# Two graph layers over a dense adjacency: layer 1's product with h by seven block products in place of eight

## The chip, the cores and the metric

The kernel runs on one core of a Trainium2 chip. The metric is the device time of one launch in microseconds (us): the median of three timed runs. One more execution was profiled; its times come from the hardware profiler. Engines: PE (TensorE, with PEld for its weight loads), DVE (VectorE), ACT (ScalarE), POOL (GpSimd), SP (SyncE, which here only issues DMAs).

## The reference, cut to what matters

16 batches of 1024 nodes with 128 features; adj is 1024 x 1024 per batch, float32. Layer 0 is one attention with a softmax and three gates; layer 1 has four heads.

```python
# layer 1, per head: h = X @ conv_w + conv_b  (1024 x 128)
scores = jnp.einsum('hbni,hij,hbmj->hbnm', h, attn_w, h)
Ah = jnp.tanh(A[None] * scores)
hh = jax.nn.relu(jnp.einsum('hbnm,hbmd->hbnd', Ah, h))   # the product with h
Xm = jax.nn.relu(jnp.mean(hh, axis=0))
return jax.nn.relu(Xm + X)
# both layers: x = layernorm(x + layer(x))
```

## The kernel before

All is float32. The main loop (L890) goes over the batches b, and for each over 32 **steps**: step = 8 * head + m, where m is a block of 128 source nodes.

Layer 1, one step (`layer1_step`, L694). PE makes the scores of block m against all 1024 target nodes in two tiles of 512 (L711, by `halves_mm`, L138, which splits a product into two of 64 weight columns). They land in PSUM buffers of the pool `ps_sc`, four deep, which all of layer 0's small products share. DVE multiplies each tile with the adjacency into `s` (L712), and ACT takes the tanh of the step's 1024 columns (L713). The product with h (`back`, L715 to L732) adds h[m]^T s into the PSUM tile `acc`, as eight products of 64 weight columns by 256 moving columns; it is issued two steps after its scores (`push`, DELAY = 2). At m = 7 `add_head` adds relu(acc) to `sum` on DVE (L745, L747).

Layer 0 of later batches is cut into named pieces, which two tables lay between the steps: BETWEEN (L872) ends layer 0 of batch b + 1, AHEAD (L877) begins that of batch b + 2. A piece's instructions go into each engine's queue after those of the step, and every queue runs in order. The pieces that matter here, with their DVE or POOL work:

- Lj loads the adjacency's block j; Ej makes its mask (POOL, L408, two buffers); Aj masks row j and takes its maximum (DVE, L425 to L433), then the exponential (ACT); Bj divides, multiplies with the adjacency (DVE, L451, L458) and issues the product of row j - 1 (`weigh`, `back`, L445 to L471).
- Sj makes scores (PE, ACT), Tj turns a row of them (DVE, then a DRAM round trip on SP: `hop`, L265).
- F, i, o are the gates (DVE reductions, POOL products with `wu_b`); I0 and O0 are eight small DVE operations each (L592, L603); V0 has the layer norm's statistics (DVE, L218 to L221) and then a power on POOL (L222); N0 normalises (DVE, L233). `turn_x1` then turns x1 for the next batch.

In a batch b >= 1, V0 stands at step 23, N0 at 24, `turn_x1` at 25, A0 to A2 at 29 to 31, and the rest of A and B in steps 31 and 0 to 10. At step 31 PE also makes the next batch's uT (`head_uT`) and half of its rows of h (`rows`, L677), which ACT copies out of `ps_sc`; at step 0 the other half. `layer1_end` finishes the output of the batch before at the steps ENDING. The adjacency of a batch is loaded once, for both layers (16 buffers).

Of the kernel before, what the change touches and what calls it, by code (L numbers as in the profile page):

```python
# [19 lines left out]
P = 128  # L20
EPS = 1e-5
# [3 lines left out]
def two_layer_adjacency_kernel(  # L25
# [28 lines left out]
    adjp = ctx.enter_context(tc.tile_pool(name="adjp", bufs=2 * NB))  # L54
    sb = ctx.enter_context(tc.tile_pool(name="sb", bufs=2))
    ps_sc = ctx.enter_context(tc.tile_pool(name="ps_sc", bufs=4, space=PSUM))
# [7 lines left out]

    warm = sb.tile([P, N], F32, tag="sum", name="warm", bufs=1)
    nc.vector.memset(warm[:, :P], 0.0)
    ident = consts.tile([P, P], F32, name="ident")
# [4 lines left out]
    a_in = sb.tile([P, P], F32, tag="hz", name="a_in", bufs=4)  # L72
    nc.scalar.dma_start(a_in, A)
    ww_in = sb.tile([P, P], F32, tag="hz", name="ww_in", bufs=4)
# [3 lines left out]
    rows_x = sb.tile([3, P], F32, tag="s1", name="rows_x", bufs=4)  # L78
# [35 lines left out]
    cw_in = sb.tile([P, H, D], F32, tag="s1", name="cw_in", bufs=4)  # L114
    cw_last = sb.tile([P, H, D], F32, tag="s1", name="cw_last", bufs=4)
    aw = sb.tile([P, H, D], F32, tag="s1", name="aw", bufs=4)
    cw = consts.tile([P, H, D], F32, name="cw")
    cwT = sb.tile([P, H, P], F32, tag="s1", name="cwT", bufs=4)
    caT = sb.tile([P, H, P], F32, tag="s1", name="caT", bufs=4)
# [4 lines left out]
    a_sym = sb.tile([P, P], F32, tag="hz", name="a_sym", bufs=4)  # L124
    s_ww = sb.tile([P, P], F32, tag="hz", name="s_ww", bufs=4)
# [3 lines left out]
    b_wide = sb.tile([P, P], F32, tag="uT1", name="b_wide")  # L129
# [7 lines left out]

    def halves_mm(out, lhsT, rhs, start, stop):  # L138
        for c in range(2):
            nc.tensor.matmul(out[ts(c, 64)], lhsT[:, ts(c, 64)], rhs, start=start, stop=stop)  # L140
# [33 lines left out]
    def join_weights():  # L174

        nc.gpsimd.memset(cw_last[0:1], 0.0)
        nc.gpsimd.tensor_sub(cw, cw_in, cw_last)
        yield
        pt = small("p_cwT")
        for hd in range(H):  # L180
            nc.tensor.transpose(pt[:, ts(hd, P)], cw[:, hd, :], ident)
        nc.scalar.copy(cwT.rearrange("p h f -> p (h f)"), pt)
        yield
        pt = small("p_caT")
        for hd in range(H):
            nc.tensor.matmul(pt[:, ts(hd, P)], aw[:, hd, :], cwT[:, hd, :], start=True, stop=True)
        nc.scalar.copy(caT.rearrange("p h f -> p (h f)"), pt)  # L187
        yield
        pt = small("p_m")
        for hd in range(H):  # L190
            nc.tensor.matmul(pt[:, ts(hd, P)], caT[:, hd, :], cwT[:, hd, :], start=True, stop=True)
        nc.scalar.copy(ms.rearrange("p h f -> p (h f)"), pt)
# [10 lines left out]
    def layernorm(t, dst, name, on_scalar=False, eps=EPS, own=False):  # L203
# [17 lines left out]
        nc.vector.tensor_scalar_add(rs, mv[:, :, 1], eps)  # L221
        nc.gpsimd.tensor_tensor(rs, rs, mhalf[:, :n], ALU.pow)  # L222
# [15 lines left out]
    def project_T(dst, w, src, bias, name, halves=range(NH), split=True):  # L238

        for q in halves:  # L240
            ps = small(f"pT_{name}_{q}")
            (halves_mm if split else nc.tensor.matmul)(
                ps, w, src[:, ts(q, 512)], start=True, stop=True
            )
            if bias is None:
# [3 lines left out]

    def project_rows(dst, w, src, bias_row, name):  # L250

        for q in range(NH):
            ps = small(f"pR_{name}_{q}")
            psv = ps.rearrange("p (k d) -> p k d", d=D)
            for k in range(BH):
                nc.tensor.matmul(psv[:, k, :], src[:, ts(q * BH + k, P)], w, start=True, stop=True)
            nc.vector.tensor_add(
                dst[:, q * BH : (q + 1) * BH, :], psv,
                bias_row.unsqueeze(1).to_broadcast([P, BH, D]),
            )  # L260
# [18 lines left out]

    def land():  # L280
        while hops:
            hops.popleft()()
# [6 lines left out]

    adj_t, x1_t, x1T_t = {}, {}, {}  # L290


    def layer0(b):
# [6 lines left out]
        mm = halves_mm if b else nc.tensor.matmul  # L300

        def load_xT():
            t["xT"] = sb.tile([P, N], F32, tag="xT", name=f"xT_{b}")
            nc.sync.dma_start(t["xT"], xT[b])

        def load_adj(j):
            a = adj_t[b, j] = adjp.tile([P, N], F32, tag="adj", name=f"adj_{b}_{j}")

            (nc.sync if b < 2 else nc.gpsimd).dma_start(a, adjT[b, ts(j, P), :])  # L309
# [5 lines left out]
        def project_q(q):  # L315
# [7 lines left out]
            if (b, q) != (0, 0):  # L323
                return project_T(t["qT"], q_w, t["xT"], c_col, f"q0_{b}", [q], split=b > 0)
# [76 lines left out]
        def find_edges(j):  # L401

            if b == 0:
                m = sb.tile([P, N], BF16, tag="h1", name=f"edge_{b}_{j}", bufs=NB + 1)
# [3 lines left out]
            engine.tensor_scalar(m, adj_t[b, j], 0.0, None, ALU.is_gt)  # L408
# [36 lines left out]
        def weigh(j):  # L445

            s = row(j)
            adj = adj_t[b, j].rearrange("p (k d) -> p k d", d=P)
            rz = sb.tile([P, 1], F32, tag="rz", name=f"rz_{b}_{j}", bufs=4)
            t["hz", j] = sb.tile([P, D], F32, tag="hz", name=f"hz_{b}_{j}", bufs=4)  # L450
# [8 lines left out]
            if j and (b or j not in (1, NB - 1)):  # L459
                back(j - 1)  # L460

        def back(j, halves=range(NH)):
            if j == 0:
                acc = ps_acc.tile([P, N], F32, tag="acc0", name=f"acc0_{b}")

                other = ps_acc.tile([P, N], F32, tag="acc1", name="acc_other") if b == 0 else acc
                t["acc"] = [acc[:, :512], other[:, 512:]]
# [11 lines left out]
        def relu():  # L479
            back(NB - 1)  # L480
            for q in range(NH):
                relu_half(q)
# [12 lines left out]
        def rows_half(q):  # L495
# [3 lines left out]
            pt = ps_acc.tile([P, N], F32, tag=f"acc{q}", name=f"pt0_{b}_{q}")  # L499
# [74 lines left out]
        def gate_f():  # L574
            sum_hp(1)
            sigmoid(t["gate"][:, :, 1:2])
            forget()
# [22 lines left out]
        def outer(p):  # L600
# [6 lines left out]
            t["norm", p] = layernorm(u[:, ks], t["x1"][:, ks, 1 : D + 1], f"0_{b}_{p}")  # L607
# [21 lines left out]
        else:  # L629
            pieces.update(R=relu, P=turn_hp, Y=partial(weigh_hp, 1), F=gate_f, i=gate_i, o=gates_io)  # L630
# [45 lines left out]

    def rows(b, ks):  # L677

        for k in ks:
            h1_t[b, k] = sb.tile([P, H * D], F32, tag="h1", name=f"h1_{b}_{k}", bufs=NB + 1)  # L680
            ps = small(f"pR1_{b}_{k}")
            halves_mm(
                ps, x1T_t[b][:, ts(k, P)], cw.rearrange("p h d -> p (h d)"), start=True, stop=True
            )
            nc.scalar.copy(h1_t[b, k], ps)  # L685

    def head_uT(b, hd, halves=range(NH)):
        if (b, hd) not in u_t:
            u_t[b, hd] = sb.tile([P, N], F32, tag="uT1", name=f"uT1_{b}_{hd}")
        project_T(u_t[b, hd], ms[:, hd, :], x1T_t[b], None, f"u1_{b}_{hd}", halves)  # L690

    acc1_t, sum_t, kept = {}, {}, []

    def layer1_step(b, hd, m):  # L694
        x1T, h1, uT = x1T_t[b], h1_t[b, m], u_t[b, hd]
        adj = adj_t[b, m]
        if m == 0:
            acc1_t[b, hd] = ps_acc.tile([P, N], F32, tag="acc1", name=f"acc1_{b}_{hd}")
        acc = acc1_t[b, hd]
# [7 lines left out]
        else:  # L707
            s = sb.tile([P, N], F32, tag="s1", name=f"s1_{b}_{hd}_{m}", bufs=4)
        for q in range(NH):
            ps = ps_sc.tile([P, 512], F32, tag="sc", name=f"sc1_{b}_{hd}_{m}_{q}")  # L710
            halves_mm(ps, x1T[:, ts(m, P)], uT[:, ts(q, 512)], start=True, stop=True)  # L711
# [3 lines left out]
        def back(halves=range(NH)):  # L715
            if len(halves) < NH:
                for q in halves:
                    halves_mm(
                        acc[:, ts(q, 512)], h1[:, ts(hd, D)], s[:, ts(q, 512)],
                        start=(m == 0), stop=(m == NB - 1),  # L720
                    )
            else:
                for d in range(2):
                    for r in range(2):
                        for c in range(NH):
                            q = (c + d) % NH
                            at = slice(q * 512 + r * 256, q * 512 + r * 256 + 256)
                            nc.tensor.matmul(  # L728
                                acc[ts(c, 64), at], h1[:, hd * D + c * 64 : hd * D + c * 64 + 64],
                                s[:, at], start=(m == 0 and r == 0), stop=(m == NB - 1),  # L730
                                skip_group_check=True,
                            )  # L732
# [33 lines left out]
    def last_back(acc, i, k, ms=range(NB)):  # L766

        for m in ms:
            nc.tensor.matmul(
                acc[:, ts(i, D)], kept[0][:, m, ts(k, P)], h1_t[B - 1, m][:, ts(H - 1, D)],  # L770
# [3 lines left out]
    def last_rows(b, acc, k0, k1):  # L774

        n, at = k1 - k0, slice(k0 - BH, k1 - BH)
        y = sb.tile([P, n, D], F32, tag="s1", name=f"y_{b}_{k0}", bufs=4)
# [9 lines left out]
    def layer1_end(b):  # L787
        x1 = x1_t[b][:, :, 1 : D + 1]
        y = sb.tile([P, NB, D], F32, tag="u", name=f"y_{b}", bufs=1)
        turn(y, sum_t[b].rearrange("p (k d) -> p k d", d=P), f"sum_{b}")  # L790
# [5 lines left out]
        yield from layernorm(y, y, f"1_{b}")  # L796
        nc.gpsimd.dma_start(out[b].rearrange("(k p) d -> p k d", p=P), y)

    def last_end(b, k0, k1):
# [3 lines left out]
        y = sb.tile([P, n, D], F32, tag="s1", name=f"y_{b}_{k0}", bufs=4)  # L803
# [13 lines left out]

    first, second, join = layer0(0), layer0(1), join_weights()
# [4 lines left out]
    run(second, "L0 L1 L2 L3 L4 L5 L6 L7")  # L823
# [36 lines left out]
    rows(0, range(0, BH - 1))  # L860
    turn_first_x1(x1_t[0], 1)
    rows(0, range(BH - 1, BH))
# [4 lines left out]
    rows(0, range(BH, NB))  # L867
    land()

# [3 lines left out]
        0: "L7 E5 B1 A3", 1: "B2", 2: "E6 A4", 3: "E7 B3 A5", 4: "A6", 5: "B4", 7: "B5 A7",  # L873
        8: "B6", 10: "B7", 11: "X R", 12: "P", 14: "Y", 16: "F", 18: "i", 20: "o", 21: "I0",
        22: "O0", 23: "V0", 24: "N0",
    }
    AHEAD = {  # L877
        9: "W", 12: "Q0 Q1", 14: "H0 h0 H1 h1 H2 h2", 15: "S0", 16: "T0 S1", 17: "T1 S2", 18: "T2 S3",
        19: "T3 S4", 20: "T4 S5", 21: "T5 S6", 22: "T6 S7", 25: "L0", 26: "L1", 27: "L2 E0",
# [96 lines left out]
```

## Time and profile before

| what | value |
|---|---|
| timed runs, us | 2415.01, 2415.14 (median), 2420.69 |
| profiled execution: its time, its span, us | 2420.78, 2419.0 |
| busy share of the span | PE 100%, DVE 64%, ACT 44%, POOL 25% |
| granted TensorE clock | 1.0 |
| one batch of the steady part (888.85 to 1037.88), us | 149.03 |
| DMA | 198.23 MB, 82 GB/s |

The busy table gives each engine's share over the whole span. The groups give, for one line of the code and one shape, the number of instructions, their total busy time and the mean of one; matmuls overlap, so the mean is longer than what one adds, which the starts of the timeline show. A float32 product stands as two PE instructions for each one that the code issues. The windows give busy time between two points of time.

### The profile page before, as it was taken

How to read it: one execution, taken by the hardware profiler on the slowest of the kernel's cores; microseconds unless marked ns; L12 is line 12 of the kernel's file. 1: busy time of each engine (PE TensorE's matmuls, PEld its weight loads, DVE VectorE, ACT ScalarE, POOL GpSimd, SP SyncE). 2: the span in 40 equal slices, each digit the busy share in tenths (PEclk: the TensorE clock that was granted, in tenths of full speed). 3: DMA queues.
4: the chain of work that ended last, by engine and by line, in shares of the span. 5: the costliest groups of instructions: out<-in, count | busy, mean ns of one | idle time of the engine just before them, and what ended most of it. 6: DMA issues, size and time to landing. Idle time of an engine off the chain costs nothing.

```text
span 2419.0 us, 39731 instructions
## 1 busy us (share of the span) xinstructions
PE 2410.0 (100%) x15747; PEld 1141.4 (47%) x15747; DVE 1551.6 (64%) x3262; ACT 1063.7 (44%) x1503; POOL 609.1 (25%) x389
## 2 busy tenths in 40 slices
PE   9999999999999999999999999999999999999999
PEld 5444444444444444454444444445444444444444
DVE  6756666666666666676566665666666576666555
ACT  6544344443444434344344454434444344443333
POOL 1314131241312413123131331312214132141000
PEclk9999999999999999999999999999999999999999
DMA  5334151341514415143242422425234252341010
GB/s 184 79 71 129 36 133 44 86 124 41 134 39 99 109 49 127 48 109 90 61 115 54 118 73 70 105 62 119 65 73 112 53 127 58 78 116 35 18 27 10
DMA packets 474269, 198.23 MB, mean 82 GB/s; under 512 B 414947, under 2 KB 440290, under 8 KB 474083
## 3 DMA queue, kind: packets, MB, share of 16 engines
q1 hardware_dynamic: 455501, 129.03, 23.1%
q0 software_dynamic: 18288, 66.59, 9.0%
q8 instruction: 124, 2.03, 0.4%
q14 instruction: 62, 0.51, 0.1%
q10 hardware_dynamic: 294, 0.07, 0.0%
HBM read 136.12 MB, written 59.51 MB: 81 GB/s over the span
## 4 chain that ended last, share of the span: by engine, by line
PE 98%; DVE 1%; DMA 0%; issue 0%; SPq 0%; ACT 0%; POOL 0%; POOLq 0%; DVEq 0%
PE sc L140 41%; PE acc L728 36%; PE acc L140 9%; PE pT_u L140 5%; PE pR L140 5%; PE pR_h L140 1%; PE pT_q L140 1%; PE sc L361 0%; PE acc L469 0%; PE acc_other L469 0%; DVE s L712 0%; DVE st L218 0%; PE idle L136 0%; DMA dram_turn<-turn 0%; DMA R<-dram_turn 0%
## 5 line engine op out<-in xcount | busy, mean ns | idle before, releaser
L712 DVE TENSOR_TENSOR s<-sc,adj 128x512 f32<-128x512 f32 x1008 | 684.6, 688 | 716.8 <-PE sc L140 694.6
L713 ACT ACTIVATE s<-s 128x1024 f32<-128x1024 f32 x504 | 533.3, 1058 | 1060.3 <-DVE s L712 900.4
L140 PE MATMUL sc<-uT,x1T 128*64 128x512 f32 x4096 | 966.5, 592 | 0.2
L728 PE MATMUL acc<-s,h 128*64 128x256 f32 x8064 | 956.3, 379 | 0.4 <-DVE sum L747 0.4
L728 PEld LDWEIGHTS acc<-s,h 128*64 128x64 f32 x8064 | 580.3, 137 | 505.6 <-issue 273.8
L140 PEld LDWEIGHTS sc<-uT,x1T 128*64 128x64 f32 x4096 | 294.3, 137 | 472.6 <-issue 359.3
L408 POOL TENSOR_SCALAR edge<-adj 128x1024 uint8<-128x1024 f32 x120 | 332.7, 2772 | 316.4 <-DVE top_None L425 313.9
L222 POOL TENSOR_TENSOR rs<-rs,mhalf 128x8 f32<-128x8 f32 (+3 forms) x35 | 54.2, 1548 | 884.9 <-DVE rs L221 884.8
L140 PE MATMUL acc<-R,hz 128*64 128x512 f32 x960 | 226.4, 592 | 0.0
L437 ACT ACTIVATE R<-R,nmax 128x1024 f32<-128x1024 f32 x126 | 144.7, 1149 | 81.2 <-DVE nmax L433 72.7
L425 DVE CUSTOM_DVE_ANT_0 R<-R,edge 128x1024 f32<-128x1024 f32 x126 | 152.8, 1213 | 0.9 <-ACT caT L187 0.4
L458 DVE TENSOR_TENSOR R<-R,adj 128x1024 f32<-128x1024 f32 (+1 forms) x127 | 152.0, 1197 | 0.0
L140 PE MATMUL sc<-xT,qT 128*64 128x512 f32 (+2 forms) x720 | 136.5, 486 | 0.0
L367 ACT ACTIVATE R<-sc,h 128x512 f32<-128x512 f32 (+1 forms) x192 | 110.9, 579 | 57.2 <-PE sc L140 44.9
L550 POOL TENSOR_TENSOR x1T<-hp,wu_b 128x1024 f32<-128x1024 f32 x45 | 106.8, 2373 | 104.4 <-DVE hws L556 63.9
L140 PE MATMUL pT_u<-x1T,ms 128*64 128x512 f32 x512 | 121.0, 592 | 0.0
L140 PE MATMUL pR<-cw,x1T 128*64 128x512 f32 x512 | 117.3, 595 | 0.0
L140 PEld LDWEIGHTS acc<-R,hz 128*64 128x64 f32 x960 | 68.9, 137 | 91.7 <-issue 76.5
L309 POOL DMA_DIRECT2D adj<-in_adjT_dram x112 | 65.9, 588 | 91.0 <-DVE s L712 91.0
L747 DVE SCALAR_TENSOR_TENSOR sum<-acc,sum 128x512 f32<-128x512 f32 x95 | 61.2, 686 | 41.4 <-PE acc L728 39.1
L685 ACT COPY h<-pR 128x512 f32<-128x512 f32 x128 | 72.3, 592 | 28.1 <-PE pR L140 26.8
L246 ACT COPY uT<-pT_u 128x512 f32<-128x512 f32 x128 | 71.4, 580 | 20.0 <-PE pT_u L140 20.0
(169 smaller groups left out, 1132.4 us busy)
## 6 DMA issues: line engine op xcount, KB each, us to landing
adj<-in_adjT_dram POOLq DMA_DIRECT2D x112, 512.0 KB, 4.1
xT<-in_xT_dram SPq DMA_DIRECT2D x16, 512.0 KB, 5.1
adj<-in_adjT_dram SPq DMA_DIRECT2D x16, 512.0 KB, 8.2
x<-in_x_dram SPq DMA_DIRECT2D x16, 512.0 KB, 5.6
dram_hp<-turn_hp SPq DMA_DIRECT2D x15, 512.0 KB, 2.6
hp<-dram_hp SPq DMA_DIRECT2D x60, 128.0 KB, 3.2
dram_x<-turn_x SPq DMA_DIRECT2D x15, 512.0 KB, 3.0
x1T<-dram_x SPq DMA_DIRECT2D x60, 128.0 KB, 6.1
```

What stands on the lines that cost most here:

```text
L140: nc.tensor.matmul(out[ts(c, 64)], lhsT[:, ts(c, 64)], rhs, start=start, stop=stop)
L246: nc.scalar.copy(dst[:, ts(q, 512)], ps)
L367: nc.scalar.activation(to, psv, AF.Identity, bias=r)
L408: engine.tensor_scalar(m, adj_t[b, j], 0.0, None, ALU.is_gt)
L425: nc.vector.tensor_tensor_reduce(to[:, ks], s[:, ks], t["edge", j][:, ks], 1.0, nmax, ALU.mult, ALU.max, top)
L437: nc.scalar.activation(row(j), row(j), AF.Exp, bias=t["nmax", j], accum_out=t["z", j])
L458: nc.vector.tensor_mul(s[:, ks], s[:, ks], adj[:, ks])
L550: nc.gpsimd.tensor_mul(t["hw"], t["hp"], wu_b[:, g : g + 1, :].to_broadcast([P, NB, D]))
L685: nc.scalar.copy(h1_t[b, k], ps)
L712: nc.vector.tensor_mul(s[:, ts(q, 512)], ps, adj[:, ts(q, 512)])
L713: nc.scalar.activation(s, s, AF.Tanh)
L728: nc.tensor.matmul(acc[ts(c, 64), at], h1[:, hd * D + c * 64 : hd * D + c * 64 + 64], s[:, at], start=(m == 0 and r == 0), stop=(m == NB - 1),
```

## The change

In all batches but the last, the steps go in pairs: block i and block i + 4 of a head (m in the order 0, 4, 1, 5, ...; step m of a head is half m % 2 of pair m // 2). The product of a pair, 2 x 2 blocks of targets, sources and feature halves, is made by seven block products (Winograd's form of Strassen's algorithm), each two matmuls of 64 by 256, in place of eight. Sums of blocks of s are made by `differ` (DVE) and two additions in `early_first` (POOL), sums of blocks of h by `join_rows` (POOL), and the seven results are put together at a head's end (`early_second`, `combine`, `sum_up`, `sum_end`). Products 3, 2, 1 ("early") of a pair are issued in the second half of the pair after it, 5, 7, 6, 4 ("late") in the first half of the one after that. Every plan of pieces is written anew. The adjacency is loaded twice: into a ring of three for layer 0, and again for layer 1 (`load_adj1`), all on SP's queue. PSUM: `ps_sc` has three buffers, `acc0` one bank, `acc1` and `acc2` two each.

```diff
-    ps_sc = ctx.enter_context(tc.tile_pool(name="ps_sc", bufs=4, space=PSUM))
+    ps_sc = ctx.enter_context(tc.tile_pool(name="ps_sc", bufs=3, space=PSUM))
...
+        if apart:
+            yield
         nc.gpsimd.tensor_tensor(rs, rs, mhalf[:, :n], ALU.pow)
...
+                a = adjp.tile([P, N], F32, tag="ring", name=f"ring_{b}_{j}", bufs=3)
+            t["adj", j] = a
+            nc.sync.dma_start(a, adjT[b, ts(j, P), :])
...
+    def join_rows(b, hd, g):
...
+        nc.gpsimd.tensor_sub(x[:, 0], a22, a21)
+        nc.gpsimd.tensor_add(x[:, 1], x[:, 0], a11)
+        nc.gpsimd.tensor_sub(x[:, 2], x[:, 1], a12)
+        nc.gpsimd.tensor_sub(a21, a11, a21)
...
+        def differ(self):
+            t = self.t
+            nc.vector.tensor_add(
+                t[:, X3 : N12 + 1 : N12 - X3, :],
+                t[:, N12 : N12 + 1, :].to_broadcast([P, 2, 512]), t[:, B22 : B11 + 1, :],
+            )
...
+            w, at = {
+                1: (h[:, 0, d1], B11), 2: (h[:, 1, d1], N21), 3: (x[:, 2], B22),
+                4: (h[:, 1, d2], N21), 5: (x[:, 0], N12), 6: (x[:, 1], B22), 7: (h[:, 0, d2], X3),
+            }[p]
+            for q in range(NH):
+                nc.tensor.matmul(
+                    out[ts(q, HD)], w, self.t[:, at, ts(q, HN)],
...
+        def early_first(self):
+            t = self.t
+            self.product(3)
+            self.product(2)
+            nc.gpsimd.tensor_add(t[:, B22], t[:, B22], t[:, N12])
+            nc.gpsimd.tensor_add(t[:, N21], t[:, B22], t[:, N21])
...
+        def combine(self):
...
+            nc.vector.tensor_sub(w[:, 1], w[:, 0], a[6])
+            nc.vector.tensor_add(w[:, 2], w[:, 1], a[7])
+            nc.vector.tensor_add(
+                w[:, 1:4:2], w[:, 1:3], a[5].unsqueeze(1).to_broadcast([P, 2, HN])
+            )
+            nc.vector.tensor_add(w[:, 2], w[:, 2], a[4])
+
+        def sum_up(self):
...
+            nc.gpsimd.tensor_add(w[:, 0:2], w[:, 0:2], w[:, 4:6])
...
+            nc.scalar.activation(four, four, AF.Relu)
+
+        def sum_end(self):
...
+            nc.gpsimd.tensor_add(sum_t[self.b], sum_t[self.b], w)
...
+        0: "E5 B4 L6", 1: "A5", 2: "E6 B5 L7", 3: "A6", 4: "E7 B6", 5: "A7", 6: "B7", 7: "R0",
+        8: "G0", 9: "G1", 10: "G2", 11: "X G3", 12: "R1 P", 14: "Y", 16: "F", 17: "f", 19: "i",
+        21: "o", 22: "I0", 23: "O0", 24: "v0 V0", 25: "N0",
     }
     AHEAD = {
...
+        9: "W", 12: "Q0 Q1", 13: "H0 h0", 14: "H1 h1 H2 h2", 15: "S0", 16: "T0 S1", 17: "T1 S2",
+        18: "T2 S3", 19: "T3 S4", 20: "T4 S5 L0", 21: "T5 S6", 22: "T6 S7 E0 L1", 23: "A0",
+        24: "E1 B0 L2", 25: "A1", 26: "E2 B1 L3", 27: "A2", 28: "E3 B2 L4", 29: "A3",
+        30: "E4 B3 L5", 31: "A4",
     }
...
+                for q in range(NH):
+                    now.score(half, q)
+                    if half == 0 and old:
+                        (old.late_second if q else old.late_first)()
+                    elif half and before:
+                        (before.early_second if q else before.early_first)()
+                    if half and q == 0 and old:
+                        old.combine()
+                now.tanh(half)
...
+            if half == 0 and before:
+                before.differ()
             land()
+            if half and old:
+                old.sum_up()
+            if half == 0 and ended:
+                ended.sum_end()
+            if b and step == 3:
+                rows(b, (2, 6, 3, 7))
+                join_rows(b, 0, 1)
...
+            if step == (26 if b else 28) and b + 1 < B:
                 turn_x1(b + 1)
             run(after, AHEAD.get(step, ""))
+            if step > H * NB - NB and b + 1 < B:
+                load_adj1(b + 1, ORDER[m - 1])
```

v0 is the part of the layer norm up to its statistics, V0 the power; f is the POOL part of F; Gp and R0, R1 are layer 0's second half of targets, now accumulated after the first half in one bank. At steps 4, 12 and 20 `head_uT` and two `join_rows` follow; at step 31 `head_uT`, four `rows` and one `join_rows`.

## The prediction, on record before the changed kernel ran

> **What bounds the kernel now.** I read the busy table first, then the groups, then one steady batch in the windows, then the timeline.
>
> ```profile
> PE 2410.0 (100%) x15747; PEld 1141.4 (47%) x15747; DVE 1551.6 (64%) x3262; ACT 1063.7 (44%) x1503; POOL 609.1 (25%) x389
> ...
> L728 PE MATMUL acc<-s,h 128*64 128x256 f32 x8064 | 956.3, 379 | 0.4 <-DVE sum L747 0.4
> ```
> ```profile
> 888.85:1037.88 149.03, 149.03 (x986) 69.86 (x984) 96.95 (x203) 65.75 (x93) 40.17 (x25) 1.00 0.34 86
> ```
>
> PE (the first column after the length) is busy for all of the batch's 149.03 us, DVE for 96.95, at a granted clock of 1.00. So the kernel is PE's instruction stream, and only less PE work shortens it, as long as nothing makes PE wait. What PE work costs is read from starts:
>
> ```profile
> 999.78 1.89 PE L140 MATMUL sc<-uT,x1T 128*64 128x512 f32 x8
> ...
> 1001.50 1.90 PE L728 MATMUL acc<-s,h 128*64 128x256 f32 x16
> ...
> 1003.22 1.89 PE L140 MATMUL acc<-R,hz 128*64 128x512 f32 x8
> ```
>
> Scores of a step: 1.72 us; product with h: 1.72 us for eight matmuls of the code, 0.215 each.
>
> **What is removed.** A pair takes 14 such matmuls in place of 16: 0.43 us. 16 pairs a batch, 15 batches: 6.88 us a batch, 103.2 us in all. With no wait 2420.8 - 103.2 = 2317.6 us. First halves of a pair (even steps) now take 3.44 us of layer-1 PE work, second halves (odd) 3.01.
>
> **What is added on DVE, and where it lies.** `differ` is not in the trace; L458 has its form (two SBUF operands, 1024 elements): 1.13 us from start to start, 16 a batch. `combine` is three operations of 256 and one of 512 elements on PSUM; L747 takes 0.69 at 512, L592 0.34 at 128, so I estimate 3 x 0.45 + 0.69 = 2.0; four a batch, in place of four pairs of `add_head` at 1.2 to 1.3. That is +18 + 8 - 5: about 118 of 142 us, still less than PE. But the pieces are not spread evenly, and three score buffers let PE lead DVE by little. The new plan puts A and B (before, mostly beside rows and second-layer products) beside I, O, V and N:
>
> ```profile
> 1066.27 2.18 DVE L592 SCALAR_TENSOR_TENSOR u<-hp,gate,u 128x128 f32<-128x128 f32 x8
> 1068.38 0.43 DVE L385 STREAM_TRANSPOSE turn<-R 128x256 f32<-128x256 f32 x1
> ...
> 1070.15 2.18 DVE L603 SCALAR_TENSOR_TENSOR u<-u,gate,x 128x128 f32<-128x128 f32 x8
> 1072.25 0.30 DVE L385 STREAM_TRANSPOSE turn<-R 128x128 f32<-128x128 f32 x1
> ...
> 1073.81 1.63 DVE L218 BATCH_NORM_STATS2 st<-u 128x6 f32<-128x128 f32 x8
> ...
> 1076.10 1.28 DVE L712 TENSOR_TENSOR s<-sc,adj 128x512 f32<-128x512 f32 x2
> 1077.98 2.14 DVE L233 TENSOR_SCALAR x<-u,mv,rs 128x128 f32<-128x128 f32 x8 [0.59 <-POOL rs L222]
> 1080.03 1.28 DVE L712 TENSOR_TENSOR s<-sc,adj 128x512 f32<-128x512 f32 x2
> ```
>
> Start to start: I0 2.11, O0 2.10, V0's statistics 2.29, N0 2.05; by further rows of the timeline the two score multiplications 1.20 back to back, Aj 1.33, Bj 1.19, turn 1.16, T6 0.22. DVE's queue in the new plan:
>
> - 22: differ, I0, T6 = 3.46
> - 23: scores, O0, A0 = 4.63
> - 24: scores, differ, v0, B0 = 5.81
> - 25: scores, N0, A1 = 4.58
> - 26: scores, differ, turn_x1, B1 = 4.68
> - 27: scores, combine, A2 = 4.53
> - 28: scores, differ, B2 = 3.52; 29: 2.53; 30: 3.52; 31: scores 1.20
>
> Sum 38.5 us, from step 22's last score multiplication to step 31's. PE needs 3.66 + 3.01 + 3.44 + 3.01 + 4.30 + 3.01 + 4.30 + 3.01 + 4.30 = 32.0 us for the same stretch (each B adds 0.86 of layer 0's product, S7 0.22). The lag, 6.4 and 0.3 that DVE brings along, reaches PE through `ps_sc`: a tile needs the buffer of three tiles before. At step 31 nothing gives it back: tanh (1.06), the copies of uT and then of four rows stand behind the last multiplication on ACT, and with three buffers PE cannot run the rows without them. So 6.7 us a batch are lost: DVE takes the bound here.
>
> **POOL.** Two additions of 512 a pair. Nearest row: L535, 128x512, 1.04 (half of L550's 2.37 is 1.19; L177, also 128x512, took 2.00). With 1.04 they take 2.1, and p6 of the same pair follows p2 by 0.86 + 0.43 + 0.86 + 0.86 + 0.86 = 3.9 us of PE work. In a plain pair they are hidden. The cover goes where POOL's queue holds something that waits. At 24 the power (1.67) waits behind v0, E1 (2.77) behind it, and the additions of step 25 behind both; PE waits in step 26, but DVE is late anyway. At 27 to 30 it adds up: combine ends 29.5 us after step 22 began, relu on ACT at 32.4 (after the tanh), `sum_end` (2.37) 34.8, E3 37.5, then the additions 39.6, and step 30's p6 waits for them, which puts its tail, step 31 and the last multiplication at 45.0 in place of 42.3: 2.7 us more. The window loses 9.4.
>
> **Elsewhere.** Step 3: combine ends 3.9 us after the step's start, `sum_up`'s addition on POOL (behind the pair's own) about 5.4, ACT's tanh 5.6, the relu 6.7; the copies of the step's rows stand behind it, so the fourth row finds no buffer: 2.0 us. `join_rows` (128 elements, 0.3 by the POOL copy of 128x128, 0.29) are 12 operations ahead of step 5's additions: 0.3. S1 behind F's exponential and step 21 behind two joins: 0.5 together. The extra ACT work (about 0.2 per uT half tile, 2 us a head) is below its slack. The second load of the adjacency is 8 x 0.5 MB a batch on SP; steps 25 to 31 then move some 6 MB in 29 us, where 169 GB/s already took a share of 0.79 at 1086 to 1104. The ring is loaded two steps (6.5 us) ahead against landings of 4.1 to 8.2; if that cover fails, E waits and the additions with it: from 0 to 3 us a batch, nothing in the sum.
>
> **Sum.** Wait of a batch: 9.4 + 2.0 + 0.8 = 12.2 against 6.88 saved: +5.3. Batches 1 to 13: +69. Batch 0, whose I to N come two steps later, and with them turn_x1 before step 31: +9 (4 more, an estimate from the 3.0 and 6.1 us of its two DMA trips). Batch 14 has no A and B (10 us of DVE less, so no lag): 2.5 - 6.9 = -4. Batch 15 has neither. 2420.8 + 74 = 2494.8 in the profiled execution; the median lies at 0.9977 of it: **2489 us**.
>
> **Two rules against the change.** From 20.02 to 22.02 L177 ran on POOL beside L425 on DVE, which ended at 20.89, and L453 on DVE (0.91, its other three 0.29) ended with it:
>
> ```profile
> 19.67 1.22 DVE L425 CUSTOM_DVE_ANT_0 row<-R,edge 128x1024 f32<-128x1024 f32 x1 [0.71 <-ACT R L367]
> ...
> 21.19 0.91 DVE L453 TENSOR_SCALAR hz<-h,rz 128x128 f32<-128x128 f32 x1
> ```
>
> But E (2.77) beside L458 and L425 at 977 to 981 lengthened neither. The Trainium skill (SBUF — State Buffer, "Who interferes with whom") says that a DVE operation with two SBUF inputs and a POOL operation that reads SBUF share a port, and one blocks. By the rule the additions would often take L177's 2.00 (the third rival); by the E row nothing. The clock stood at 1.00 in every window but the last 4 us, after PE's end: 0.75. The skill (TensorE: Matmul & The Clock Gate, "Why this matters for your kernels") warns of PE gaps over some 3 us. By it the wait in step 26, 3 to 4 us, could cost 1.7 us more in each of 13 batches, +22; the trace before has no such gap.
>
> **The rivals.**
> - *DVE keeps up* (the other side: faster). Place: steps 22 to 31. If the 38.5 us are at most 34, because neighbouring small operations overlap more than in the rows used, the lag stays within PE's lead and 3 us of waits remain: 2420.8 - 103.2 + 45 = 2362.6, as a median 2357. It decides from a wait below 6.88 a batch. For it: DVE has 24 us to spare over the batch. Against: start-to-start times already contain the overlap.
> - *Even.* Only the DVE lag stays, POOL and step 3 are hidden: wait 6 to 8, 2405 to 2430.
> - *POOL is the bound.* The additions take 2.00: 4.0 a pair against 3.9, so nearly every pair waits, and the window by some 3 more: wait about 20, 2420.8 + 13 x 13.1 + 13 = 2604, as a median 2598.
> - *It doesn't do what it says* (as many PE instructions as before): none, the matmul is written with 64 x 256.
>
> **Chances.** Forecast 0.52 (waits of 9 to 16: 2440 to 2545), POOL 0.14, even 0.14, faster 0.20. A measurement here tells 0.3% (7 us) from no change. The even case gives 0.03 faster, 0.08 same, 0.03 slower: faster 0.23, same 0.08, slower 0.69. Both signs hold much, so the range runs from a faster case with 5 us of waits (2385) to the POOL one (2590); 0.2 lies outside.
>
> **What would show it.** Right: fewer product instructions by an eighth with starts 0.107 us apart; PE idle in steps 23 to 31, released by DVE score multiplications and by POOL's additions; DVE without a gap there; a wait at step 3 for a copy of rows; batches of about 154 us. Wrong: batches below 147 us, DVE idle between steps 24 and 29, or PE idle spread over all pairs.

## The result and the profile after

The changed kernel takes **2799.99 us** (median of 4 runs, 2792.80 to 2803.65) against 2415.2 for the kernel before: a ratio of 1.158, with a 95% interval of 1.156 to 1.161. I had forecast 2489 and a range up to 2590: slower, but by a fifth of what it is. The profiled execution took 2799.67 us, with a span of 2797.9.

The busy table, and the groups of the page that answer to those shown of before (columns: count | busy us, mean ns | idle time before them, and what ended most of it):

```profile
PE 2466.4 (88%) x14537; PEld 1076.3 (38%) x14537; DVE 2088.8 (75%) x3622; ACT 1161.7 (42%) x1827; POOL 1728.0 (62%) x1343
...
L850 POOL TENSOR_TENSOR pair<-pair 128x512 f32<-128x512 f32 x240 | 331.4, 1381 | 444.8 <-PE early L832 406.6
...
L832 PE MATMUL late<-pair,hx 128*64 128x256 f32 x1920 | 310.4, 402 | 199.5 <-POOL pair L850 151.1
...
L450 POOL TENSOR_SCALAR edge<-ring 128x1024 uint8<-128x1024 f32 x120 | 376.8, 3141 | 69.0 <-DMA ring<-in_adjT_dram 53.1
L809 DVE TENSOR_TENSOR pair<-pair 128x1024 f32<-128x1024 f32 x240 | 375.9, 1566 | 0.0
L832 PE MATMUL late<-pair,h 128*64 128x256 f32 x1920 | 317.2, 410 | 53.6 <-POOL pair L851 53.5
```

PE, at 100% before, is at 88%, and no engine has taken its place: DVE is at 75%, POOL at 62%. PE has 1210 instructions fewer: 960 are the seven products (6720 in place of 7680), the rest the same work in wider matmuls at the start and in the last batch. Yet it is busy for longer than before (2410.0). A steady batch, in the same view as before (length; busy us and count of PE, PEld, DVE, ACT, POOL; granted clock; DMA share; GB/s):

```profile
939.00:1113.40 174.40, 153.36 (x922) 67.17 (x920) 131.68 (x228) 72.17 (x112) 114.73 (x88) 0.94 0.34 94
```

174.4 us in place of 149.0, PE idle for 21, and a granted clock of 0.94 in place of 1.00. PE's longest waits of that batch, by start (in brackets how long PE was idle before the row, and what ended it):

```profile
965.08 1.08 PE L74 MATMUL pR<-cw,x1T 128*64 128x512 f32 x4 [1.43 <-ACT h L755]
982.99 1.12 PE L832 MATMUL late<-pair,hx 128*64 128x256 f32 x4 [5.22 <-POOL pair L850]
...
1073.16 1.08 PE L832 MATMUL late<-pair,hx 128*64 128x256 f32 x4 [3.65 <-POOL pair L850]
1075.38 1.12 PE L832 MATMUL late<-pair,h 128*64 128x256 f32 x4 [1.14 <-POOL pair L851]
1085.82 0.65 PE L832 MATMUL late<-pair,hx 128*64 128x256 f32 x4 [1.89 <-POOL pair L850]
...
1096.92 0.95 PE L832 MATMUL late<-pair,hx 128*64 128x256 f32 x4 [2.84 <-DVE w L875]
```

These are steps 3, 6, 24, 26 and 28. Product 6 (p6), and p4 behind it, waits for POOL's additions at 6, 24 and 26, and p5 for `combine` at 28; the score multiplications, which I had expected to hold PE, release 8.9 us of waits in the whole run.

**Where the 482 us went.** Without any wait the forecast was 2317.6. PE's matmuls at full clock are 2410.0 - 103.2 = 2306.8; they took 2466.4, **159.6 us more**. By the trace's record PE was busy for 239.1 us while it was granted one half of the clock; half of that, **119.6 us, is slow clock**. The other 40.0 goes with the waits: a product's matmul takes 0.38 us and the next starts 0.21 after it, so at each of PE's 241 gaps some 0.17 us of a matmul's end is no longer hidden behind the next one. Outside PE's busy time lie 333.3 us of the profiled execution, 10.8 of which the kernel before has too: **322.5 us are waits**.

### The profile page after: what moved, and what is told of

Its sections match the earlier page's. It is cut to its first block, busy times and chain, and to the rows that moved or that the text cites. A ratio compares the mean times of both kernels' runs of the same rounds, so it can differ in the third digit from the quotient of the medians.

```text
span 2797.9 us, 39657 instructions
## 1 busy us (share of the span) xinstructions
PE 2466.4 (88%) x14537; PEld 1076.3 (38%) x14537; DVE 2088.8 (75%) x3622; ACT 1161.7 (42%) x1827; POOL 1728.0 (62%) x1343
## 4 chain that ended last, share of the span: by engine, by line
PE 53%; DVE 23%; POOL 14%; issue 5%; ACT 3%; DMA 1%; SPq 0%; POOLq 0%; DVEq 0%; ACTq 0%
PE sc L74 23%; PE late L832 9%; PE acc L74 8%; PE early L832 6%; DVE R L467 4%; DVE pair L809 3%; DVE pair L798 3%; POOL pair L851 3%; DVE pair L800 3%; POOL edge L450 3%; POOL pair L850 2%; DVE x L246 2%; PE pR L74 2%; PE pT_u L74 2%; DVE R L500 2%
## 5 line engine op out<-in xcount | busy, mean ns | idle before, releaser
L805 ACT ACTIVATE pair<-pair 128x1024 f32<-128x1024 f32 x480 | 508.3, 1059 | 969.5 <-DVE pair L798 628.1
L850 POOL TENSOR_TENSOR pair<-pair 128x512 f32<-128x512 f32 x240 | 331.4, 1381 | 444.8 <-PE early L832 406.6
L798 DVE SCALAR_TENSOR_TENSOR pair<-sc,adj 128x512 f32<-128x512 f32 x480 | 323.0, 681 | 285.8 <-PE sc L74 285.7
L800 DVE TENSOR_TENSOR pair<-sc,adj 128x512 f32<-128x512 f32 x480 | 318.1, 683 | 283.3 <-PE sc L74 277.7
L832 PE MATMUL late<-pair,hx 128*64 128x256 f32 x1920 | 310.4, 402 | 199.5 <-POOL pair L850 151.1
L450 POOL TENSOR_SCALAR edge<-ring 128x1024 uint8<-128x1024 f32 x120 | 376.8, 3141 | 69.0 <-DMA ring<-in_adjT_dram 53.1
L809 DVE TENSOR_TENSOR pair<-pair 128x1024 f32<-128x1024 f32 x240 | 375.9, 1566 | 0.0
L832 PE MATMUL late<-pair,h 128*64 128x256 f32 x1920 | 317.2, 410 | 53.6 <-POOL pair L851 53.5
L851 POOL TENSOR_TENSOR pair<-pair 128x512 f32<-128x512 f32 x240 | 340.3, 1418 | 18.8
L832 PE MATMUL early<-pair,h 128*64 128x256 f32 x1920 | 294.0, 385 | 0.0
L74 PE MATMUL acc<-R,h 128*64 128x512 f32 x960 | 260.1, 644 | 0.6 <-DVE R L500 0.4
```

Of the source, the lines that this page charges most:

```text
L74: nc.tensor.matmul(out[ts(c, HD)], lhsT[:, ts(c, HD)], rhs, start=start, stop=stop)
L450: engine.tensor_scalar(m, t["adj", j], 0.0, None, ALU.is_gt)
L798: nc.vector.scalar_tensor_tensor(to, psv, -1.0, adj, op0=ALU.mult, op1=ALU.mult)
L800: nc.vector.tensor_mul(to, psv, adj)
L805: nc.scalar.activation(s, s, AF.Tanh)
L809: nc.vector.tensor_add(t[:, X3 : N12 + 1 : N12 - X3, :], t[:, N12 : N12 + 1, :].to_broadcast([P, 2, 512]), t[:, B22 : B11 + 1, :],)
```

## The experiments

For each kernel below, "PE longer" is PE's busy time over 2306.8, "slow clock" half of the time for which PE was busy at one half of the clock, and "PE idle" the span less PE's busy time, all from the profile. Unless said otherwise a time is one run, beside a run of the kernel before on the same chip (2416.3 to 2421.0).

| kernel | time | PE longer | slow clock | PE idle | DVE busy |
|---|---|---|---|---|---|
| after | 2800.0 | 159.6 | 119.6 | 331.5 | 2088.8 |
| no_adds | 2591.3 | 62.3 | 43.6 | 220.4 | 1955.3 |
| no_edge | 2669.6 | 107.6 | 72.5 | 253.3 | 2035.1 |
| no_adds_edge | 2532.1 | 60.4 | 46.9 | 163.1 | 1889.3 |
| adds_dve | 2787.3 | 150.3 | 93.5 | 328.4 | 2312.8 |
| pool_order | 2753.0 | 116.2 | 83.1 | 328.2 | 2136.6 |
| order_no_edge | 2697.2 | 84.6 | 52.7 | 304.0 | 2101.7 |
| order_no_adds | 2569.6 | 65.1 | 49.3 | 195.9 | 1957.0 |
| chain_early | 2933.6 | 187.5 | 130.3 | 437.5 | 2141.0 |
| order_chain | 2764.5 | 126.7 | 85.6 | 329.2 | 2109.1 |
| order_edge_norm | 2584.8 | 72.5 | 36.9 | 203.7 | 1952.2 |
| order_all | 2581.2 | 68.8 | 37.4 | 209.0 | 1962.6 |

Rows of waits, below, give who waited for what: us in total, times, longest us. In the code cuts several entries of a table stand on one line.

My theory after the result: POOL's two additions cost the most, as they stand in its queue behind masks, joins and the power, and as DVE's operations lengthen beside them; the slow clock follows from the gaps. The rival was my forecast's: DVE's load in steps 22 to 31 is the bound, whatever POOL does.

**no_adds**: `early_first` without its additions. Products 6 and 4 then use unfinished sums, so this kernel computes something else.

```
-            nc.gpsimd.tensor_add(t[:, B22], t[:, B22], t[:, N12])
-            nc.gpsimd.tensor_add(t[:, N21], t[:, B22], t[:, N21])
```

> Leaves out the two additions of early_first on POOL, so products 6 and 4 take unfinished sums. POOL theory (PE waits for these additions, and the granted clock falls behind the waits): the 205 us that PE's rows show behind L850 and L851 go, and most of the slow clock: about 2480 us (2440 to 2560), clock 0.98 or more. DVE-lag theory, as in the prediction: only what POOL adds goes, some 3 us a batch and its clock: 2730 or more, and PE then waits for score multiplications in steps 23 to 31.

Measured 2591.3, between the two: 209 us of the loss go with the additions, and 170 over the kernel before stay. What PE then waits for:

```profile
PE late L832 <- DVE w L872: 65.3, 18, 4.3
PE sc L74 <- DVE pair L800: 43.0, 28, 2.6
PE sc L74 <- DVE pair L798: 42.4, 18, 3.5
```

That is DVE's lag: 85 us at the score multiplications, where I forecast it, and 65 at `combine`, where I did not. In the kernel after it was mostly hidden (8.9 and 48.3 us): PE waited for POOL first, and DVE caught up meanwhile.

**no_edge**: no mask E; A takes the adjacency, whose entries are 0 and 1 here, as the mask itself.

```
+            if b:
+                t["edge", j] = t["adj", j].rearrange("p (k d) -> p k d", d=P)
+                return
```

> Leaves out the mask E of layer 0 from batch 1 on: A takes the adjacency itself, which holds only 0 and 1. Queue theory (the additions are late because other POOL work, E above all, stands before them): PE's wait behind L850 and L851 falls by more than half, 2620 us (2570 to 2680). Port theory (the additions and DVE's operations stretch each other): the stretched times of differ (1.57) and of A stay, 2740 us or more.

Measured 2669.6, in the band of the queue theory: 130 us less, with the waits for the additions down from 204.6 to 78 us, though each still takes 1.38 and 1.36. So most of the waiting for POOL is its queue, not the length of an addition.

**filler**: in batches from the second on, matmuls without use, into columns of `early` that nothing reads, ahead of the second half of step 6's, 24's and 26's late products (24, 20 and 10 of them).

```
+                    if q and b and step in FILL:
+                        filler(b, hd if m > 3 else hd - 1, FILL[step])
```

> Adds matmuls into unused PSUM columns ahead of products 6 and 4 in steps 6, 24 and 26 (5.2, 4.3 and 2.2 us at full clock), where PE waits 5.4, 4.8 and 2.6 us. Clock theory (the waits pull the granted clock to a half, which costs some 140 us): clock 0.98 or more, 2690 us (2660 to 2730). If the slow clock costs nothing, because it falls into waits: 2800 us or more.

Measured 2772.1, between the two. The clock rose from 0.950 to 0.978, but the extra matmuls took part of what that gave, and the 4.4 us at step 28 stayed. It doesn't price the clock by itself.

**before_adds**: the kernel before, with two additions of 512 on POOL in every second step, on a tile of their own. To make room, xT has one buffer in place of two, which may also cost some time at the start.

```
+        if m % 2 and b + 1 < B:
+            for _ in range(2):
+                nc.gpsimd.tensor_add(dead[:, 0], dead[:, 0], dead[:, 1])
```

> The kernel before with two additions of 128x512 on POOL every second step, on a tile of their own that nobody waits for (xT has one buffer in place of two to make room, which costs some us at the start). Port theory: the additions take over 1.27 us on average, and L458 (1.206), L425 (1.213) and L233 (0.34) get longer by a tenth or more, while PE stays the bound: 2415 to 2440 us. Without a shared port: these rows stay within 2%.

Measured 2476.0, above the 2415 to 2440 expected, though PE depends on none of these additions. Its DVE groups (the mask's row was 1213 before, x's norm 351, L458 1206):

```profile
L425 DVE CUSTOM_DVE_ANT_0 R<-R,edge 128x1024 f32<-128x1024 f32 x126 | 202.4, 1606 | 0.7 <-ACT caT L187 0.4 <-ACT cwT L182 0.3
L458 DVE TENSOR_TENSOR R<-R,adj 128x1024 f32<-128x1024 f32 x125 | 153.5, 1228 | 0.0
L233 DVE TENSOR_SCALAR x<-u,mv,rs 128x128 f32<-128x128 f32 x128 | 72.3, 633 | 9.9 <-POOL rs L222 9.7
```

DVE's busy time grew from 1551.6 to 1666.0 with no operation added to it: this is the lengthening, without a queue of POOL that PE waits for. The mask and the norm are longer by far more than the tenth expected, L458 by 2% only: half of its operations have no POOL operation beside them here, and those took 1.20 to 1.22. PE is idle for 56 us (9 before), 31 of them for DVE's `sum`; which operation made that late I did not trace.

**pool_order**: the same operations, with POOL's long ones behind a pair's additions and not ahead of them, and the ring's first loads out of SP's queue of turns.

```
-        20: "T4 S5 L0", 22: "T6 S7 E0 L1", 24: "E1 B0 L2", 26: "E2 B1 L3",
+        8: "L0", 10: "L1", 11: "L2 E0", 23: "A0 E1", 25: "A1 E2 L3",
...
-            if half == 0 and ended:
+            if m == 5 and ended:
...
-                for g in range(2):
-                    join_rows(b, hd + 1, g)
+            elif hd < H - 1 and m in (5, 7):
+                join_rows(b, hd + 1, m // 2 - 2)
```

> The same operations, only in another order on the queues: masks E one step earlier, in odd steps, so that they stand behind a pair's two POOL additions and not ahead of them; the ring's first three loads at steps 8 to 11 instead of 20 to 24; join_rows split over steps 5 and 7 behind the additions; the power at 25 behind E2; sum_end at step 5. Theory order (the lost time is mostly POOL's queue, in which the additions stand behind operations that are long or that wait): PE's idle time released by POOL falls from 204 us to under 60, the waits of 5.2 at step 6 and 3.7 at step 24 go, the DVE lag shows in their place as it did without the additions: 2560 to 2640. Theory capacity (POOL and its port are too slow in any order): the waits for POOL only move to other pairs, 2720 or more.

Measured 2753.0. The waits for POOL went, from 204.6 to 8 us, as the theory of the order says; the time did not, and that theory fell. Its waits:

```profile
PE late L832 <- DVE w L875: 99.9, 17, 6.8
PE sc L74 <- ACT R L407: 84.9, 31, 4.4
PE sc L74 <- DVE pair L798: 34.8, 31, 5.8
```

PE now waits for DVE, or for ACT operations behind one of DVE's, and is idle as long as in the kernel after (328 us): the additions beside them keep DVE late, as order_no_adds shows below.

**chain_early** moved layer 0's chain up to two steps earlier, from its second half's product (G) over the gates to the norm, to lighten DVE in steps 23 to 28 (shown: the table's last entries):

```
-        21: "o", 22: "I0", 23: "O0", 24: "v0 V0", 25: "N0",
+        19: "o", 20: "I0", 21: "O0", 22: "v0 V0", 23: "N0",
```

> Only layer 0's chain of gates and norm is moved two steps earlier (I0, O0, statistics, N0 at 20 to 23 in place of 22 to 25), so that DVE has less to do in steps 23 to 28; POOL's work keeps its order but for the parts of that chain. Theory order (POOL's queue holds PE up, and DVE's lag hides behind that): little, 2720 to 2800. Theory DVE (DVE's 38.5 us in steps 22 to 31 are the bound, as I forecast): 90 us or more come back, under 2710.

Neither: 2933.6. Waits for POOL are still 179 us, and new ones came at the copies of layer 0's scores (50) and at the PSUM buffers into which uT is made (33). I read this from the waits and tested it no further.

**order_chain**: pool_order and chain_early together, with step 3's row copies ahead of the relu and uT at step 29.

> Both of the other two edits together, and the two waits for ACT taken away (step 3's row copies ahead of the relu, the next batch's uT at step 29 in place of 31). If the loss is queue order on POOL, DVE and ACT, and the slow clock only follows from the gaps, waits of 3 to 8 us a batch stay, the clock is above 0.99, and the time is 2370 to 2480. If DVE's operations that the additions stretch and POOL's load of about 115 us a batch hold PE up in any order: 2550 or more.

2764.5: the second theory. The longest wait moved to `sc` behind DVE's L798 (108.3 us, up to 6.4).

**no_adds_edge**: neither additions nor masks.

> The kernel after without the two additions on POOL (two of the seven products then use unfinished sums) and without the masks E (the adjacency itself is the mask). POOL keeps its other work. The DVE lag of steps 22 to 31 that I forecast (6.7 us a batch, with 2 at step 3 and 1 elsewhere) would now stand alone, with unstretched DVE operations: 2440 to 2520, PE idle at steps 24 to 28 released by DVE, clock over 0.98. If it stays near 2591, as without the additions alone, the masks cost DVE nothing and the lag is larger than I forecast.

2532.1, just above the forecast band.

```profile
PE 2367.2 (94%) x14537; PEld 1081.9 (43%) x14537; DVE 1889.3 (75%) x3622; ACT 1159.6 (46%) x1827; POOL 679.9 (27%) x743
```
```profile
PE late L834 <- DVE w L874: 58.1, 17, 4.3
PE sc L74 <- DVE pair L800: 33.2, 16, 2.6
```

PE is idle for 163 us (9 of which the kernel before has too), against the 177 of waits in my forecast. DVE does the operations of the kernel after in 1889.3 us in place of 2088.8: **200 us, 13 a batch, are lengthening beside the additions and masks**. What lengthening stays has POOL's other sums beside it: `differ` takes 1.21 on average in the 171 cases with no POOL operation beside it, 1.84 in the other 69.

**adds_dve**: the additions on DVE in place of POOL, after the step's score multiplications.

```
-            nc.gpsimd.tensor_add(t[:, B22], t[:, B22], t[:, N12])
-            nc.gpsimd.tensor_add(t[:, N21], t[:, B22], t[:, N21])
...
+                now.tanh(half)
+                if half and before:
+                    before.add_on()
```

> The two additions of a pair run on DVE, after the odd step's score multiplications, in place of POOL; nothing else changes. DVE gets some 2 x 0.6 us a pair, 288 us in all (half of the 1.21 of L500 for half as many elements), on top of the 1955 it had without the additions. Theory queue and port (the additions cost what they cost because they stand in POOL's queue and because DVE's operations lengthen beside them): faster than the kernel after although DVE is the busier engine: five pairs in steps 22 to 31 add 6 us of lag a batch to the 2591 without the additions, 2660 to 2750, no wait for POOL, DVE's mask operation near 1.33. Theory DVE alone (DVE's load is the bound, the stretch beside POOL is a detail): over 2800.

2787.3, between the two. No wait for POOL is left, and the mask is back at 1.26; but the additions take 0.91 and 0.78 on DVE where I had expected 0.6, and DVE is busy for 2312.8 us. On either engine the additions cost about the same.

**order_no_edge** and **order_no_adds**: pool_order without the masks, and without the additions.

> The kernel with POOL's queue in the other order (2753), without the masks E: the adjacency, whose entries are 0 and 1, is its own mask. If DVE's lengthening beside POOL holds that order up, the mask operation falls from 1.65 to 1.4 and DVE's busy time from 2137 to 2050 or less, and the waits at steps 22 and 28 (4.4 and 6.8) get shorter: 2590 to 2680. If the additions alone keep DVE late, 2700 or more.

2697.2: above the band, just below the other theory's 2700. The mask operation only fell to 1.56, DVE's busy time to 2101.7, and the two waits stayed at 4.6 (for the copy of step 22's score) and 6.8. So the additions, far more than the masks, keep DVE late.

> The kernel with POOL's queue in the other order, without the two additions (two of the seven products then use unfinished sums). With the additions that order took the waits for POOL away (204 to 8 us) and put waits for DVE in their place. Theory port: those were made by DVE operations lengthened beside the additions, so they shrink to what the kernel after without additions has (4.3 at step 28): 2530 to 2600. If the order itself, with its later masks and norm, makes DVE late: 2650 or more.

2569.6, in the band: without the additions this order is the better one (2591.3 in the other).

**order_edge_norm**: order_no_edge with the two norms on ACT, one operation of scale and bias for each block; `turn_x1` stands a step later and one part of `layer1_end` a step earlier.

```
+                nc.scalar.activation(
+                    dst[:, k, :], t[:, k, :], AF.Identity, bias=mv[:, k, 0:1],
+                    scale=rs[:, k : k + 1],
+                )
```

> The order without masks, and both normalisations (8 operations each) on ACT in place of DVE: 2.7 us and more of DVE a batch less at step 26, and as much at step 14. Theory DVE lag: 40 to 80 us faster than the order without masks alone, 2540 to 2620, still slower than the kernel before, since combine, the differences and A, B, I, O stay. If ACT's extra 2.4 us ahead of its tanh is what PE waits for then, no faster than that one.

2584.8: taking some 150 us from DVE gave 112, more than I had expected, and the waits for `combine` fell from 100.9 to 25.3. In this order DVE's load is what counts most. The largest waits left:

```profile
PE sc L74 <- ACT R L417: 63.7, 18, 4.6
PE sc L74 <- DVE pair L810: 27.2, 17, 4.5
```

**order_all**: four more waits taken away by order alone (median of 4 runs).

```
+            if 16 <= step <= 22:
+                run(after, AHEAD.get(step, ""))
             run(nxt, plan.get(step, ""))
...
+                if m == (NB - 2 if b else NB - 1):
+                    head_uT(b + 1, 0)
```

> The kernel with POOL's order, without masks and with norms on ACT (2584.8), and four waits taken away by order alone: at steps 16 to 22 layer 0's scores and turns stand ahead of the gates (the last score's copy stood on ACT behind a tanh that waited 3.4 us for I0: PE 4.6 us), step 3's row copies ahead of the relu (1.4), the next batch's uT at step 30 in place of 31 (1.8), the end of layer 0's product two steps behind its last multiplication (0.7). If the waits are what keeps the saving away: 13 batches x some 7.5 us less, 98, and half of the slow clock's 46 with it: 2440 to 2480, the clock above 0.985. If DVE's lag beside POOL simply shows at the next place: 2530 or more.

2581.2, a ratio of 1.067 (1.066 to 1.069) to before: the waits moved.

```profile
PE sc L74 <- DVE pair L810: 97.3, 45, 5.5
...
PE sc L74 <- ACT R L417: 3.8, 3, 2.0
```

The wait for ACT went from 63.7 to 3.8 us, and the one for DVE's score multiplications grew from 27.2 to 97.3. No version of the change that I ran, whole or with parts left out, came near the kernel before, and the fastest of them leave out masks that the kernel before still makes.

## Why the prediction was wrong, point by point

- **What is removed**: right. 960 product instructions fewer, an eighth. In no_adds_edge PE is busy for 2367.2 us; less 46.9 of slow clock and some 0.17 for each of its 104 gaps that is 2303 against my 2306.8.
- **combine**: right (2.0 forecast; 0.41 + 0.42 + 0.69 + 0.42 = 1.94). `differ` has 1.21 alone, as L458 had, but 1.57 on average.
- **POOL: the first step that failed.** The sum had 3.0 us of waits a batch for it (2.7 at step 30, 0.3 at step 6); PE's waits for the additions came to 204.6 in the run, 13.7 in a mean batch (batches 2 to 13). I priced an addition at 1.04 from L535; it takes 1.25 at least and 1.38 and 1.42 on average. That still hides in a plain pair, as I wrote. What I mis-sized is the queue ahead of it. "`join_rows` ... ahead of step 5's additions: 0.3" is the 5.22 us at step 6: E7 took 3.75 there (2.77 in the kernel before), and eight joins of 0.46 and more, priced at 0.3, stood behind it. "PE waits in step 26, but DVE is late anyway" was wrong twice: the waits are at 24 (4.8) and 26 (2.6), and DVE doesn't hold PE there, since PE is held before it. And the ring, of which I put "nothing in the sum": L0 stood behind the turns in SP's queue until 1063.48, and E0, with the additions behind it, until 1068.98, which is the wait at step 24. (The row names DVE's L654, which ended in the same moment; E0 reads the ring's block, which landed at 1068.9.) DVE, for which I had named "without a gap there" as the sign, waits 2.68 us for that mask:

```profile
1063.48 0.38 SPq L349 DMA_DIRECT2D ring<-in_adjT_dram  x1
...
1068.98 2.89 POOL L450 TENSOR_SCALAR edge<-ring 128x1024 uint8<-128x1024 f32 x1 [6.42 <-DVE u L654]
...
1071.86 1.25 POOL L850 TENSOR_TENSOR pair<-pair 128x512 f32<-128x512 f32 x1
1071.91 2.28 DVE L467 CUSTOM_DVE_ANT_0 R<-R,edge 128x1024 f32<-128x1024 f32 x1 [2.68 <-POOL edge L450]
1073.16 1.08 PE L832 MATMUL late<-pair,hx 128*64 128x256 f32 x4 [3.65 <-POOL pair L850]
1073.19 2.14 POOL L851 TENSOR_TENSOR pair<-pair 128x512 f32<-128x512 f32 x1
```

- **The port: the second step that failed**: "by the E row nothing". The row of L177 was the one to take. In the rows above, A's mask takes 2.28 beside L850 where it took 1.21 before, and L851 takes 2.14 beside that mask where it takes 1.26 at its shortest. The Trainium skill (SBUF — State Buffer, "Who interferes with whom") says that one side holds the shared port for its whole instruction while the other blocks. For the additions these rows agree (for E they don't, see below): the mask ends 1.08 us after L850's end and L851 1.14 after the mask's, each nearly its whole length alone. The score multiplications, which read PSUM and one SBUF tile, agree too: they stayed at 0.68. `differ` takes 1.20 to 1.22 in the 75 cases with no POOL operation beside it, 1.73 on average in the other 165. Over the run it is the 200 us of DVE above. I also took a lucky moment for a rule. E beside L458 lengthened nothing at 977 to 981, and nor did any E of the kernel before: all 75 operations of A and B beside one began 1.2 us or more after its start. One that begins with E does wait, as in the kernel after at 1087:

```profile
977.23 2.77 POOL L408 TENSOR_SCALAR edge<-adj 128x1024 uint8<-128x1024 f32 x1 [10.91 <-DVE top_None L425]
...
978.52 1.21 DVE L458 TENSOR_TENSOR R<-R,adj 128x1024 f32<-128x1024 f32 x1
```
```profile
1087.07 2.77 POOL L450 TENSOR_SCALAR edge<-ring 128x1024 uint8<-128x1024 f32 x1
...
1087.11 2.08 DVE L467 CUSTOM_DVE_ANT_0 R<-R,edge 128x1024 f32<-128x1024 f32 x1
```

  Without the additions B takes 1.41 with the masks (no_adds) and 1.23 without them (no_adds_edge).
- **The DVE lag**: about the right size in the wrong kernel, and in part at another place. In no_adds_edge, where little lengthens DVE, PE waits 10.0 us in a mean batch, 8.5 of it in steps 24 to 31 and 1.43 at step 3; I had forecast 9.5 (6.7 for the lag, 2.0 at step 3, 0.8 elsewhere). But 3.9 of it is at step 28, where p5 of the next head needs the PSUM tile that `combine` still reads: the sum has no term for that wait. The score multiplications hold PE for 2.5. In the kernel after the lag hid behind POOL, but for 3.0 at step 28; with POOL in order (pool_order) it came back larger, 6.8 there.
- **The clock: the third step that failed**: 22 us at most and not in the sum, against 119.6 measured. The gap of 3 to 4 us that I foresaw at one place came at several, and shorter ones cost something too (below). The 40.0 us of matmul ends at PE's gaps had no term either.
- Sum: the profiled execution is 304.9 us above my 2494.8; 119.6 of that is the clock, 40.0 the matmul ends, and 145.3 are waits (322.5 against 177.2).
- The rival *POOL is the bound* named the engine that PE waited for most, not the mechanism: 62 and 72 of the 240 pairs wait for the two additions, not nearly every pair, and with those waits gone the time falls by only 47 us.

**What is shown, and what is not.** Shown: taking away the additions gives 209 us, the masks 130, both together 268; reordering POOL alone gives 47 and turns its waits into waits for DVE. Without both, 116 us over the kernel before remain, so the rest of the change (its work on DVE and ACT, POOL's other sums, one score buffer less, the second load) already costs more than the 103 it saves. Which part of the rest costs how much was not measured: `ps_sc` had three buffers in every version. Not shown either: that no order could pass 2415. A version that spreads A and B over other steps was not tried.

## What to carry to other kernels

When an engine at 100% gets less work and its neighbours get more, price the neighbours with both running: durations read from a trace in which POOL was idle three quarters of the time don't hold when it is busy. Write POOL's and SP's queues out step by step, as for DVE, and ask of each instruction on which PE depends what stands ahead of it and what that one waits for. And price gaps of PE with the clock that they cost, not by their length alone.

## What the runs showed of the hardware

- **Gaps of PE and the granted clock.** Before, the clock was below 1.00 once, for 4.1 us at the end, after PE's last matmul; after, in 58 stretches, nearly all of 3.4 or 6.8 us at one half, 282.8 us in all. In them a product's matmuls start 0.42 us apart in place of 0.21. I set PE's gaps beside the clock's record, counting a gap as followed when such a stretch begins after the gap's start and at most 8 us after its end. In the kernel after that holds for 26 of 26 gaps over 3 us, 37 of 61 between 1.5 and 3, and 3 of 36 between 0.7 and 1.5. Over that kernel and the experiments it is 274 of 295, 202 of 530 and 60 of 660. Of the gaps that stand alone (no other over 0.5 us in the 10 us before or the 8 us after) it is 76 of 77, 46 of 134 and 1 of 360. The Trainium skill (TensorE: Matmul & The Clock Gate, "Why this matters for your kernels") puts the limit at some 3 us. Here that is where a gap nearly always costs; of the lone gaps of 1.5 to 3 us a third were followed by a slow stretch too.
- **What holds DVE up beside POOL, and for how long.** I took A's mask, B's product and `differ` (1024 elements, two SBUF inputs) from seven traces (before, after, before_adds, no_adds, pool_order, adds_dve, order_no_adds). All 1211 with no POOL operation beside them took 1.16 to 1.23 us. All 171 that began while an addition of 512 ran at its own length (under 1.3 us) ended 2.34 to 2.44 us after the addition's start, wherever they began: they waited for its end. Beside an E at its own length (2.77) the 145 that began in its first 0.9 us took 1.23 to 2.08, the 306 that began later 1.16 to 1.22. So E held DVE up in its first microsecond or so only, not for its whole length as the profile gives it.
- **One-input operations of DVE beside POOL.** The eight norms of N0, which read one SBUF tile each, took 5.41 us beside POOL's E1 and two additions (2.77, 1.29 and 1.26 us), where they took 2.14 before:

```profile
1081.78 5.41 DVE L246 TENSOR_SCALAR x<-u,mv,rs 128x128 f32<-128x128 f32 x8
```

- **Small POOL operations.** An addition of 128 elements takes 0.46 us, one of 512 takes 1.25, one of 1024 takes 2.37: a line through them leaves 0.1 to 0.2 us for none at all, as an estimate.
